# Eight-step, full-width products of x, with their shares kept in DRAM, for the GRU of a two-layer kernel

## The chip, the cores and the metric

The kernel runs on one core of a Trainium2 chip. The time is the device time of one execution in microseconds. Five engines work side by side, each on its own instruction stream: TensorE (PE in the profile, with its weight loads as PEld), VectorE (DVE), ScalarE (ACT), GpSimd (POOL) and SyncE (SP), which issues most DMA transfers.

## The reference

Two recurrent layers with residual additions, all in f32. The input x is 64 batches x 128 steps x 512 features, and a condition of 512 features belongs to each batch.

```python
# layer 0: gated linear recurrence, in closed form
f = sigmoid(x @ W_f.T + b_f);  i = sigmoid(x @ W_i.T + b_i)
f, i = f / (f + i + EPS), i / (f + i + EPS)
new = i * (x @ W_h.T + b_h)
log_cum = cumsum(log(f + EPS), axis=1)            # along the steps
scaling = exp(log_cum[:, -1:, :] - shifted_by_one(log_cum))
x = x + cumsum(scaling * new, axis=1) + exp(log_cum) * cond[:, None, :]

# layer 1: GRU, conditioned on cond
vz, vr, vh = cond @ C_z + b_z, cond @ C_r + b_r, cond @ C + b
def step(h, xt):
    z = sigmoid(xt @ W_z + h @ U_z + vz)
    r = sigmoid(xt @ W_r + h @ U_r + vr)
    hh = tanh(xt @ W + (r * h) @ U + vh)
    return (1 - z) * h + z * hh                   # from h = 0, output at every step
x = x + scan(step, x)
```

## The kernel before

**First layer.** 16 groups of four batches, and for each group four chunks of 128 features. TensorE forms the three gates of a chunk as 128-column matmuls over 512 tokens (`gate`, line 187). VectorE then divides, multiplies and scans along the steps. GpSimd adds the result to x (`add_hidden`), and SP writes it to the DRAM tiles `x2d`.

**Second layer.** The 64 batches are two streams of 32. A step of one stream has 32 batches as stationary columns, so one matmul uses a quarter of TensorE's width; four of them, for the four quarters q of the output features, stand side by side in four strips of 32 columns (`matmuls`, line 374). In a step (`Stream.step`, line 739) the bank `g` already holds the part of the three gates that comes from x and the condition. TensorE adds the r and z gates of the state (lines 749 to 754: one pass over 256 columns), ScalarE takes the sigmoid (755), VectorE multiplies r by h and transposes in 32x32 blocks (756, 757), TensorE adds the third gate (776), ScalarE takes the tanh (784), VectorE forms the new h and its transpose (791 to 799). The two streams alternate on TensorE, with stream 1 two steps behind.

**The x part.** Where `direct(st, t)` holds (the first 8 steps of stream 0, the first 4 of stream 1) `x_products` multiplies x by the weights in full. The other steps are done four at a time with fewer multiplications: the four steps and the feature halves make a 2x2 block product, done with seven multiplications instead of eight, and each of the seven is again a 2x2 block product of seven. This needs sums of blocks of x (`gather` puts them in `sums_to_take`, and GpSimd works them off at line 625) and differences of weights (line 420). `Outer` is one of the seven outer products; a `product` (line 542) is one inner product: four matmuls side by side in the four strips, 96 columns each. Of the seven inner products one lands in a small PSUM place (`spots`) that two blocks share (line 479), one in a spot that three blocks share (line 492), and results are carried on within the bank by ScalarE copies (487, 503). VectorE adds the shared part (516) and the outer terms (532), and the finished shares of four steps wait in SBUF (`xz`) until `put_share` (line 722) copies one to `g`. In the first groups some outer products are formed without the inner level (`plain`).

**Order.** Every compute instruction is pinned: the engines execute in the order of the program text. The loop at line 954 calls the steps of both streams in turn; `slots` says in which step an outer product begins, `first_visit` stands after the r and z gates of a step and `second_visit` after its third gate. Where a step has no products, `idle_products` multiplies zeros (line 630). DMA transfers go through SP's queue in the order in which the scheduler puts them: windows of eight steps of x (`load_window`, line 675: four transfers for each stream) and outputs (line 821: four transfers for four steps, in rows of 32 features). The features of a quarter are interleaved: quarter q holds features 128 j + 32 q + c.

Of the kernel before, what the change touches and what calls it, by code (L numbers as in the profile page):

```python
# [11 lines left out]
ALU = mybir.AluOpType  # L12
# [6 lines left out]
def kernel(  # L19
# [35 lines left out]

    nc = tc.nc
# [11 lines left out]
    HP = P // 2  # L68
# [33 lines left out]
    for tb in range(K):  # L102
        load_x(0, tb, tag="h", bufs=5)
    bias0 = const.tile([3 * K, P], F32, name="bias0")
# [97 lines left out]
    def add_hidden(g, c, x2=None, ts=slice(0, S)):  # L202
# [14 lines left out]
        if g == NG - 1 and ts.start == 0:  # L217
            pin(nc.scalar.copy(streams[1].windows[0][:, c, NG // 2 - 1], x2[:, : TW * GB]))
        return added

    def sums(g, c, ts=None):

        h, i = hidden[g, c], is_[c % 2]
        if ts is not None:
            h, i = by_batch(h)[:, :, ts], by_batch(i)[:, :, ts]
        return pin(nc.gpsimd.tensor_tensor(h, i, h, ALU.add))
# [27 lines left out]
    def chunk_norm(g, c, between=None):  # L254

        f, i = fs[c % 2], is_[c % 2]
        h = work.tile([P, NP], F32, tag="h", bufs=5, name=f"h_{g}_{c}")
# [11 lines left out]
        if g > 0 or c > 0:  # L269
            before = (g, c - 1) if c else (g - 1, K - 1)  # L270
            beside += [sums(*before), add_hidden(*before)]
# [39 lines left out]
    GATES = range(3)  # L311

    def load_weights(name, ws, tag):

        t = wpool.tile([P, K, 3, D], F32, tag=tag, name=name)
        for n, w in enumerate(ws):
            nc.sync.dma_start(t[:, :, n, :], w.rearrange("(k p) e -> p k e", p=P))
        return t

    def part(w, q):  # L320

        return w.rearrange("p g (j q c) -> p g j q c", q=Q, c=C)[:, :, :, q, :]
# [3 lines left out]
    def conditioning():  # L326

        for n, b_ in enumerate((b_r, b_z, b)):
            for q in range(Q):
                rows = b_.rearrange("(j q c) -> q j c", q=Q, c=C)[q]  # L330
                nc.sync.dma_start(
                    bias1[q * SB : (q + 1) * SB, n].rearrange("p (j c) -> p j c", c=C),
                    rows.partition_broadcast(SB),
                )
        cw = load_weights("cw", (C_r, C_z, C_h), "wa")
        ps = [psum.tile([P, 3, P], F32, tag="tp", name=f"pv{s}") for s in range(2)]
        for s in range(2):
            for k in range(K):
                for j in range(K):
                    for q in range(Q):  # L340
                        pin(
                            nc.tensor.matmul(
                                ps[s][q * SB : (q + 1) * SB, :, j * C : (j + 1) * C],
                                lhsT=condT[:, k, s * SB : (s + 1) * SB],
                                rhs=part(cw[:, k], q)[:, :, j],
                                start=(k == 0 and j == 0),
                                stop=(k == K - 1),
                                skip_group_check=True,
                            )
                        )  # L350
        vs = []
        for s in range(2):
            whole = const.tile([P, 3, P], F32, name=f"whole_v{s}")
            pin(nc.vector.tensor_tensor(whole, ps[s], bias1, ALU.add))

            v = const.tile([P, 3, HP], F32, name=f"v{s}")
            pin(nc.vector.tensor_tensor(v, whole[:, :, HP:], whole[:, :, :HP], ALU.subtract))
            vs.append((whole, v))
# [3 lines left out]
    RZ, HH = slice(0, 2), slice(2, 3)  # L362
    TW = 8
    HC = K // 2
    out_parts = out.rearrange("b t (j q c) -> q b t j c", q=Q, c=C)

    def matmuls(p, lhsT, w, start=True, stop=True, half=False):

        if half:
            p = p.rearrange("p g j c -> p g (j c)")  # L370
# [13 lines left out]
    def winograd_weights():  # L384
# [8 lines left out]
        quads = [((b11[k], b12[k]), (b21[k], b22[k]), t[:, :, k]) for k in range(HC)]  # L393
        return (b11, b21, b22, t1, t2, t3, t4), iter([d for q_ in quads for d in differences(*q_)])

    def differences(b1, b2, t):

        (b11, b12), (b21, b22) = b1, b2
        t1, t2, t3, t4 = (t[:, n] for n in range(4)) if not isinstance(t, list) else t
        return [(t1, b12, b11), (t2, b22, t1), (t3, b22, b12), (t4, b21, t2)]  # L400

    def quarters(w_):

        return [[w_[k][:, :, j * P : (j + 1) * P] for j in range(2)] for k in range(HC)]
# [8 lines left out]
    def take_inner(n, t):  # L413

        inner_weights[n] = t
        return differences(*quarters(w_products[OPERANDS[n][1]]), t)
# [4 lines left out]

    class Outer:
# [3 lines left out]
        count = 0  # L426

        def __init__(self, st, group, n, inner):
            self.st, self.group, self.n, self.inner = st, group, n, inner
            self.left, w_n = OPERANDS[n]  # L430
            self.w = quarters(w_products[w_n])
            if inner:
                self.t = inner_weights[n]
            self.r = banks[Outer.count % len(banks)]
            Outer.count += 1
            st.need_sums(group, self.left[0] == "s")

        def a(self, m, k):

            st, cols = self.st, slice(k * SB, (k + 1) * SB)  # L440
            if self.left[0] == "s":
                return st.s4[:, self.left[1], m, cols]
            _, i, j = self.left
            return st.x4[self.group % 2][:, 2 * i + m, j * HP : (j + 1) * HP][:, cols]

        def s(self, n):
            left = self.left
            return self.st.ss[:, n, 4 + left[1] if left[0] == "s" else 2 * left[1] + left[2]]

        def at(self, m, j):  # L450
            return self.r[:, m, :, j, :]

        def spot(self):
            spots.append(spots.pop(0))
            return spots[-1]

        def plain(self, m):
            for k in range(HC):
                matmuls(
                    self.r[:, m], lambda _: self.a(m, k), [self.whole_w(k)],  # L460
                    start=(m == 0 and k == 0), stop=(k == HC - 1), half=True,
                )

        def whole_w(self, k):
            return w_products[OPERANDS[self.n][1]][k]

        def first(self):
            self.common = None  # L470
            if not self.inner:
                return self.plain(0)
            self.p = self.spot()
            product(self.p, self.a(0, 0), self.w[0][0], start=True)

        def copy_first(self):
            if self.inner:
                p = self.p.unsqueeze(2).to_broadcast([P, 3, 2, C])
                pin(nc.scalar.copy(self.r[:, 0], p))  # L479

        def second(self):
            if self.inner:
                product(self.at(0, 1), self.s(1), self.t[1])

        def copy_second(self):
            if self.inner:
                pin(nc.scalar.copy(self.at(1, 0), self.at(0, 1)))

        def copy_shared(self, place):
            commons.append(commons.pop(0))  # L490
            self.common = commons[-1]
# [517 lines left out]
```

## Time and profile before

| | us |
|---|---|
| median of 3 runs (2013.69 to 2016.28) | 2015.03 |
| the profiled execution's own time | 2013.68 |
| its span | 2011.9 |
| the GRU's first matmul starts at | 711.2 |
| TensorE busy from 800 to 1975 us | 1132 of 1175 |
| VectorE busy from 800 to 1975 us | 760 |
| ScalarE busy from 800 to 1975 us | 580 |
| GpSimd busy from 800 to 1975 us | 708 |

The granted TensorE clock is 1.00 in every stage. An f32 matmul appears as two records of TensorE and two of its weight load. Matmuls are pipelined and the ends of their records are modelled, so that records overlap: the pace of TensorE is read from the starts. "issue" beside an idle time means that the engine waited for nothing that the profile shows.

### The profile page before, as it was taken

To read this page: it belongs to the slowest core of one execution; us is meant where nothing else is said; L and a number is where in the kernel's file an instruction comes from. 1 tells how busy PE (TensorE), PEld (TensorE's weight loads), DVE (VectorE), ACT (ScalarE), POOL (GpSimd) and SP (SyncE) were. 2 spreads that over 40 slices of the span, in tenths; PEclk is the share of its full clock that TensorE was granted. 3 is DMA by queue.
4 is the path that set the end of the run, shared out by engine and by line. 5 is a ranking of instruction groups with operands and counts; after the bars stand their busy time and mean duration, and the time that the engine had idled before them with its cause. 6 is when DMAs were issued, how large, how long until landed. Compare 5 with 4: busy or idle time off the path is not lost.

```text
span 2011.9 us, 96221 instructions
## 1 busy us (share of the span) xinstructions
PE 1949.9 (97%) x42665; PEld 1408.7 (70%) x42665; DVE 1486.9 (74%) x2992; ACT 765.9 (38%) x2770; POOL 940.8 (47%) x1824
## 2 busy tenths in 40 slices
PE   9999999999999989999999999999999999999998
PEld 5444444444444446888888888888888889888886
DVE  6899999999999965666666666666666666666664
ACT  3122121221222222554445454444554445544442
POOL 1222222222222244656665666566656655656562
DMA  6411111211111220211211212112112111120111
GB/s 203 154 48 47 42 53 44 77 53 42 48 47 47 54 41 11 38 25 31 41 26 26 40 21 35 27 30 41 26 31 36 30 26 32 25 40 15 20 20 19
DMA packets 295064, 86.15 MB, mean 43 GB/s; under 512 B 272044, under 2 KB 272056, under 8 KB 294648
## 3 DMA queue, kind: packets, MB, share of 16 engines
q1 hardware_dynamic: 294048, 79.92, 17.7%
q8 instruction: 335, 5.49, 1.2%
q14 instruction: 81, 0.66, 0.1%
q10 hardware_dynamic: 600, 0.07, 0.0%
HBM read 46.41 MB, written 33.55 MB: 40 GB/s over the span
## 4 chain that ended last, share of the span: by engine, by line
PE 71%; DVE 22%; issue 3%; POOL 2%; ACT 1%; DMA 1%; DVEq 0%; ACTq 0%; SPq 0%; POOLq 0%
PE g L374 35%; PE bank L542 17%; PE p L187 12%; DVE h L260 7%; PE spots L542 6%; DVE h L309 2%; DVE i L292 2%; DVE h L299 2%; DVE i L291 1%; DVE i L304 1%; DVE f L276 1%; DVE h L259 1%; DVE i L279 1%; PE bank L374 1%; POOL ss L625 1%
## 5 line engine op out<-in xcount | busy, mean ns | idle before, releaser
L187 PE MATMUL p<-xT,W 128*128 128x512 f32 (+1 forms) x1560 | 670.8, 586 | 2.1 <-ACT xT L146 1.7
L374 PE MATMUL g<-w_s,h 128*32 128x256 f32 x8128 | 521.1, 380 | 14.8 <-issue 11.9
L187 PEld LDWEIGHTS p<-xT,W 128*128 128x128 f32 x1560 | 289.7, 190 | 344.8 <-issue 334.7
L374 PEld LDWEIGHTS g<-w_s,h 128*32 128x32 f32 x8128 | 324.4, 110 | 108.4 <-issue 29.8
L374 PE MATMUL g<-w_s,f 128*32 128x128 f32 x8128 | 297.0, 273 | 16.4 <-issue 10.8
L756 DVE TENSOR_TENSOR f<-f,h 128x128 f32<-128x128 f32 x254 | 74.3, 292 | 294.3 <-ACT f L755 294.3
L542 PE MATMUL bank<-w_inner,ss 128*32 128x96 f32 x5712 | 267.4, 247 | 9.9 <-issue 6.3
L374 PEld LDWEIGHTS g<-w_s,f 128*32 128x32 f32 x8128 | 236.4, 110 | 29.4 <-issue 21.0
L264 POOL COPY first<-condT 128x4 f32<-128x4 f32 x64 | 12.1, 190 | 519.1 <-DVE h L259 504.1
L260 DVE RECIPROCAL h<-h 128x517 f32<-128x517 f32 x64 | 217.0, 3391 | 2.2
L759 POOL TENSOR_SCALAR f<-f 128x128 f32<-128x128 f32 x254 | 75.7, 298 | 303.4 <-DVE f L756 303.4
L278 ACT ACTIVATE f<-f 128x512 f32<-128x512 f32 x64 | 40.4, 631 | 448.3 <-DVE f L276 448.3
L801 POOL TENSOR_TENSOR o<-o,h 128x128 f32<-128x128 f32 x254 | 115.9, 456 | 200.7 <-DVE h L797 192.0
L542 PEld LDWEIGHTS bank<-w_inner,ss 128*32 128x32 f32 x5712 | 190.1, 110 | 19.9 <-POOL ss L625 10.0
L479 ACT COPY bank<-spots 128x192 f32<-128x192 f32 x416 | 131.0, 315 | 147.9 <-PE spots L542 122.3
L755 ACT ACTIVATE f<-g 128x256 f32<-128x256 f32 x254 | 97.4, 384 | 231.4 <-PE g L374 227.7
L784 ACT ACTIVATE h<-g 128x128 f32<-128x128 f32 x256 | 71.0, 277 | 282.6 <-PE g L374 282.6
L532 DVE TENSOR_TENSOR W<-bank,W 128x384 f32<-128x384 f32 x305 | 169.6, 557 | 10.4
L791 DVE TENSOR_TENSOR h<-h,f 128x128 f32<-128x128 f32 x254 | 85.1, 335 | 110.1 <-ACT h L784 109.5
L542 PE MATMUL spots<-w_inner,ss 128*32 128x96 f32 x2856 | 129.8, 246 | 0.3 <-issue 0.3
L760 POOL TENSOR_TENSOR f<-f,h 128x128 f32<-128x128 f32 x254 | 117.0, 461 | 21.2
L722 ACT COPY g<-W 128x384 f32<-128x384 f32 x244 | 123.7, 507 | 0.2
(142 smaller groups left out, 3738.7 us busy)
## 6 DMA issues: line engine op xcount, KB each, us to landing
x<-in_x_dram SPq DMA_DIRECT2D x64, 256.0 KB, 3.0
x2d<-x SPq DMA_DIRECT2D x63, 256.0 KB, 2.0
xw<-x2d SPq DMA_DIRECT2D x124, 128.0 KB, 4.3
out_dram<-o SPq DMA_DIRECT2D x248, 64.0 KB, 2.1
w_rows<-in_L_cond_W_f_dram SPq DMA_DIRECT2D x4, 256.0 KB, 5.1
w_rows<-in_L_cond_W_i_dram SPq DMA_DIRECT2D x4, 256.0 KB, 5.9
w_rows<-in_L_cond_W_h_dram SPq DMA_DIRECT2D x4, 256.0 KB, 5.5
w_s<-in_L_cond_U_r_dram SPq DMA_DIRECT2D x1, 1024.0 KB
```

What stands on the lines that cost most here:

```text
L187: nc.tensor.matmul(p[:, tokens], lhsT=W0[:, c, n, k, :], rhs=xT[g][:, k, tokens], start=(k == 0), stop=(k == K - 1),)
L260: pin(nc.vector.reciprocal(h, h))
L374: nc.tensor.matmul(p[q * SB : (q + 1) * SB], lhsT=lhsT(k), rhs=part(wk, q), start=(start and k == 0), stop=(stop and k == len(w) - 1), ski ...
L479: pin(nc.scalar.copy(self.r[:, 0], p))
L532: pin(nc.vector.tensor_tensor(dst, r, other, ALU.add))
L542: nc.tensor.matmul(out_[q * SB : (q + 1) * SB], lhsT=a, rhs=w_[:, :, q * C : (q + 1) * C], start=start, stop=True, skip_group_check=True,)
L722: pin(nc.scalar.copy(self.g, self.xz[:, t // 2 % 2, t % 2]))
L755: pin(nc.scalar.activation(rz, g[:, RZ], AF.Sigmoid))
L759: pin(nc.gpsimd.tensor_scalar(r, z, -1.0, 1.0, ALU.mult, ALU.add))
L760: pin(nc.gpsimd.tensor_tensor(r, r, h_, ALU.mult))
L791: pin(nc.vector.tensor_tensor(hh, hh, z, ALU.mult))
L801: pin(nc.gpsimd.tensor_tensor(o, o, h, ALU.add))
```

## The change

The products of x are cut differently. A group is now eight steps of all 64 batches: two halves of four steps by two halves of the features, and within each the same again. A block has 2 steps x 64 batches = 128 stationary columns, so an inner product is one matmul of full width, 128 x 384, instead of four in strips. Each of the four output blocks of an outer product has a PSUM bank of its own, and one more bank takes the shared part. Seven inner products p1 to p7 run through the banks as a chain: p1, p3 and p5 are each copied on to the next bank by ScalarE, and p2 is the shared one.

Output rows of a block are now (2 steps x 64 batches), while a step needs (4 quarters x 32 batches), so VectorE leaves finished shares in SBUF, SP stores them to DRAM, and each step loads its own share again one step ahead. `place` puts products into the steps until a target number is reached: once after the r and z gates, once after the third gate, and no second link of one chain in the same place. `idle_products` and `plain` are gone. The direct steps become 12 and 8.

In a step r and z are two passes of 128 columns with a sigmoid each. The output is added in transposed form by GpSimd, and is transposed back in the next step. Features of a quarter are now adjacent (128 q + e), which changes how weights, biases, x and outputs are loaded and stored. A window of x now covers both streams and takes 32 transfers. The piece of the last group's first window that comes from the last chunks goes from SBUF to SBUF by DMA instead of by ScalarE.

```diff
     def add_hidden(g, c, x2=None, ts=slice(0, S)):
...
         if g == NG - 1 and ts.start == 0:
-            pin(nc.scalar.copy(streams[1].windows[0][:, c, NG // 2 - 1], x2[:, : TW * GB]))
+            for j in range(K):
+                nc.sync.dma_start(
+                    windows[0, 1][j][c * C : (c + 1) * C, NG - 1], x2[j * C : (j + 1) * C, : TW * GB]
+                )
...
     def part(w, q):
-        return w.rearrange("p g (j q c) -> p g j q c", q=Q, c=C)[:, :, :, q, :]
+        return w[:, :, q * P : (q + 1) * P]
...
+    def load_window(w, s=None, groups=None):
+        first_, n = (0, NG) if s is None else (s * NG // 2, groups or NG // 2)
+        windows[w, s] = []
+        for j in range(K):
+            t = work.tile([P, NG, TW * GB], F32, tag="xw", bufs=4, name=f"xw{w}_{s}_{j}")
+            windows[w, s].append(t)
+            for s_ in range(2):
+                a, b_ = max(first_, s_ * NG // 2), min(first_ + n, (s_ + 1) * NG // 2)
+                if a >= b_:
+                    continue
+                for q in range(Q):
+                    nc.sync.dma_start(t[q * C : (q + 1) * C, a:b_], x2d[s_][...])
...
     class Outer:
...
-    def product(out_, a, w_, start=False):
-        for q in range(Q):
-            pin(nc.tensor.matmul(out_[q * SB : (q + 1) * SB], lhsT=a, rhs=w_[:, :, q * C : (q + 1) * C], ...))
+        def product(self, bank, a, w_, start=False):
+            pin(nc.tensor.matmul(banks[bank], lhsT=a, rhs=w_, start=start, stop=True, skip_group_check=True))
+
+        def continued(self, to, of):
+            def copy():
+                self.free(to)
+                pin(nc.scalar.copy(banks[to], banks[of]))
...
+            to_copy.append(copy)
...
+        def products(self):
...
+            def p1():
+                self.free((0, 0))
...
+                self.product((0, 0), self.a(0, 0), w_[0][0], start=True)
+                self.continued((0, 1), (0, 0))
+            def p3():
+                self.product((0, 1), self.s(1), t[1])
+                self.continued((1, 0), (0, 1))
...
+        def read(self, block):
...
+            if j == 1 or block == (1, 1):
+                pin(nc.vector.tensor_tensor(r, r, self.common, ALU.add))
...
+            pin(nc.vector.tensor_tensor(dst, r, other, ALU.add))
...
+    def place(target):
+        chained = set()
+        while state["placed"] < target and ahead:
+            o, f, chain = ahead[0]
+            if chain and o in chained:
+                break
+            ahead.pop(0)
+            f()
+            if chain:
+                chained.add(o)
+            state["placed"] += 1
...
     def direct(st, t):
-        return t < (8 if st.s == 0 else 4)
+        return t < (12 if st.s == 0 else 8)
...
+        def load_share(self, t):
+            self.share = work.tile([P, 3 * P], F32, tag="xz", bufs=2, name=f"xz{self.s}_{t}")
+            rows = shares_d[t // TW % len(shares_d)][t % TW, self.s]
+            nc.sync.dma_start(self.share, rows.rearrange("q b e -> (q b) e"))
...
     def step(self, t, ...):
+            copies()
+            if t + 1 < S and not direct(self, t + 1):
+                self.load_share(t + 1)
+            while to_store:
+                to_store.pop(0)()
...
-                matmuls(g[:, RZ], ..., [w_s[:, k, RZ] for k in range(K)], start=False)
-                pin(nc.scalar.activation(rz, g[:, RZ], AF.Sigmoid))
+                of_state(0, hT_)
+                of_state(1, hT_)
+                pin(nc.scalar.activation(r, g[:, 0], AF.Sigmoid))
                 pin(nc.vector.tensor_tensor(rh, r, h_, ALU.mult))
                 pin(nc.vector.transpose(rhT, rh))
+                pin(nc.scalar.activation(z, g[:, 1], AF.Sigmoid))
...
+            read(len(to_read))
...
+            place(targets[0])
...
-                matmuls(g[:, HH], ...)
-                idle_products(idle[1])
-            second_visit()
+                of_state(2, rhT)
+            copies()
+            place(targets[1])
             pin(nc.scalar.activation(hh, g[:, 2], AF.Tanh))
...
+    GOALS = ((7, 0), (15, 35), (26, 84), (16 * (NX - 1) - 6, 7 * 7 * (NX - 1) - 14), (16 * (NX - 1) + 2, 7 * 7 * (NX - 1)))
```

## The prediction

> **What bounds the kernel now.** I read the page first: shares of the engines, then the chain that ended last, then the costliest groups.
>
> ```profile
> span 2011.9 us, 96221 instructions
> PE 1949.9 (97%) x42665; PEld 1408.7 (70%) x42665; DVE 1486.9 (74%) x2992; ACT 765.9 (38%) x2770; POOL 940.8 (47%) x1824
> ...
> PE 71%; DVE 22%; issue 3%; POOL 2%; ACT 1%; DMA 1%; DVEq 0%; ACTq 0%; SPq 0%; POOLq 0%
> ```
>
> DVE's 22% is the first layer (its scans and reciprocals, to about 711 us), which the diff leaves alone. From 711 us on (1301 us, the GRU) the chain is TensorE alone, so I read that stage in order of time. A row of the timeline is start, length, engine, line, operation and count; the count is of records, two for each f32 matmul.
>
> ```profile
> 1304.84 0.38 PE L374 MATMUL g<-w_s,h 128*32 128x256 f32 x1
> ...
> 1306.56 0.57 PE L542 MATMUL bank<-w_inner,s 128*32 128x96 f32 x13
> ...
> 1307.84 0.29 PE L542 MATMUL bank<-w_x,ss 128*32 128x96 f32 x4
> ...
> 1308.01 0.29 PE L542 MATMUL bank<-w_x,s 128*32 128x96 f32 x4
> ...
> 1308.17 0.29 PE L542 MATMUL bank<-w_inner,ss 128*32 128x96 f32 x4
> ```
>
> Starts tell the pace, since ends overlap. The r and z gates of a step take 1306.56 - 1304.84 = 1.72 us; one product of x (four 32-column matmuls side by side) takes 0.165 us (1307.84, 1308.01, 1308.17); the third gate takes 0.88 us in the same way (1303.63 to 1304.51). A bare stream would be the same: the first layer's full-width matmul of 512 columns starts every 429 ns a record, so four strips of 96 columns side by side need 4 x 2 x 96 x 0.838 / 4 = 161 ns. Column strips already run four at once at 97% of the array's pace; using all 128 columns in one matmul has almost nothing left to win there.
>
> What TensorE loses is elsewhere, in stalls with no waiter:
>
> ```profile
> 1314.09 0.66 PE L374 MATMUL g<-w_s,h 128*32 128x256 f32 x8
> 1316.42 0.85 PE L374 MATMUL g<-w_s,h 128*32 128x256 f32 x12 [1.66 <-issue]
> ```
>
> From 800 to 1975 us there are 50 pauses over 0.6 us between TensorE instructions, 43 us together, and nearly every one has a 16 KB packet of the instruction queue that began 0.4 to 2.4 us before it. I read them as TensorE waiting for its own instructions.
>
> **The change, part by part.** Streaming work of TensorE in the second stage, by the paces above:
>
> - State gates: r and z become two passes of 128 columns instead of one of 256. 254 x 3 x 0.88 = 670.6 for 254 x (1.72 + 0.88) = 660.4: +10.2 us. In return r's sigmoid can start a pass earlier, which matters only where TensorE waits (the tail).
> - Direct x products: 12 + 8 steps instead of 8 + 4. Eight more at 2.58 us (741.14 to 743.72): +20.6 us.
> - Products: 416 inner blocks x 7 = 2912 at 0.1655 us, 11 plain blocks at 1.30 us and 116 idle matmuls (9.4 us) go, 505.6 us. 15 groups x 49 = 735 matmuls of 128 x 384 come, each 2 x 429 x 384/512 = 644 ns: 473.3 us. -32.3 us.
> - Three matmuls that preset banks: +1.9 us. Sum of streaming: +0.4 us. The same multiplications, differently shaped.
>
> **Switching width** is the new cost. Before, TensorE works in 32-column strips throughout the second stage. After, the state's gates stay in strips and the products are full width, placed after r/z and again after the third gate. In the order in which the changed kernel's instructions stand there are 468 runs of full-width products (209 of one, 251 of two, 8 of three), each between strips: 936 switches. The trace has one clean switch each way, with no unmet wait beside it:
>
> ```profile
> 63.67 0.87 PE L342 MATMUL pv<-cw,condT 128*32 128x96 f32 x31
> 64.46 0.70 PE L187 MATMUL p<-xT,W 128*128 128x512 f32 x1
> ...
> 64.46 0.30 PEld L187 LDWEIGHTS p<-xT,W 128*128 128x128 f32 x2
> ...
> 709.84 1.45 PE L187 MATMUL p<-xT,W 128*128 128x512 f32 x3
> 711.22 0.85 PE L374 MATMUL g<-w_s,zeros 128*32 128x384 f32 x8
> ```
>
> Strips to full: the last strips start at 64.28 and, at 82 ns a set, the next could start at 64.36. The full matmul starts at 64.46 together with its weight load, and its record is 0.70 instead of 0.59 long: the load is not hidden, streaming begins about 64.57. Loss 0.21 us. Full to strips: the last full one starts at 710.69, is through at 711.12, and the strips, whose second set follows at 711.56 one 0.32 us stream later, began at 711.24. Loss 0.12 us. A pair costs 0.33 us, 468 pairs 154 us.
>
> [...] Bounds: nothing[...] and 0.5 us a pair (234 us), if each switch waits out a whole 0.25 us strip record.
>
> **Instruction supply.** TensorE falls from 21,487 to 14,381 matmuls, each four instructions, and the densest stretch (16 instructions in 0.165 us) is gone. The stage's pauses (43 us) fall at least with the count (-36%, -16) and at most vanish (-43). I take -28.
>
> **Work moved off TensorE's path.** Per step DVE reads 630 blocks of 128x384 at 557 ns in all (351 us; before 427 x 557 + 416 x 343 ns = 380); ScalarE has 420 bank copies of some 507 ns (213 us) for 1664 of 232 to 315 (429 us); GpSimd's sums stay near 1.7 us a step. None reaches the 5.3 us that a step will take, so the work is covered by TensorE. Its order is not: a chain of seven products now holds three copies from bank to bank, and a product waits for the copy of the one before. The copy stands in ScalarE's queue ahead of r's sigmoid or the tanh, and can first need a bank read on DVE (two instructions, 1.1 us). From r's last matmul the third gate's input is ready in 1.0 us (sigmoid 0.28, product 0.29, transpose 0.31, hand-overs); TensorE gets there after 0.88 + 0.21 + 0.64 to 1.29 + 0.12 us, so 0.85 to 1.5 us are to spare. The gate loses up to 0.3 us where such a read is forced, on fewer than half the steps: 0 to 60 us, I take 12.
>
> **DMA.** SP issued 553 transfers, now 1462: each share is stored (128 x 1.5 KB) and loaded again per step, and a window comes as 32 transfers instead of 8.
>
> ```profile
> 1308.51 3.92 SPq L675 DMA_DIRECT2D xw<-x2d  x4
> ...
> xw<-x2d SPq DMA_DIRECT2D x124, 128.0 KB, 4.3
> out_dram<-o SPq DMA_DIRECT2D x248, 64.0 KB, 2.1
> ```
>
> A share is asked for at a step's start and copied to PSUM by ScalarE at its end, some 4 us later, against about 2 us to land. Queued behind it on SP are stores and window pieces; ahead of it too. If it is late, ScalarE's copy blocks the other stream's sigmoid, then its third gate. Eight small window pieces stand between two share loads, at some 0.4 us each 3.2 us. Range 0 to 42 us (1.5 us twice in each of 14 windows), I take 5. [...]
>
> **Junction and tail.** The last group's first window now goes SBUF to SBUF by DMA (2 us) and through 8 gathers before the first product of stream 1, where TensorE already waited 1.3 us: +3. Products end 12 paired steps before the end of stream 0, where each leaves about 0.5 us idle: +6; the three lone steps shorten by 1 us each, since r no longer waits for z: -3. Leaving out idle matmuls could drop the clock, which every stage shows at 1.00: [...] a lone step's longest pause here is 2003.25 - 2001.49 = 1.8 us: nothing[...].
>
> **Sum.** 0.4 + 154 - 28 + 12 + 5 + 6 = 149 us on the profiled execution's own 2013.7 (span 2011.9 and 1.8 around it), 2163; the median shown, 2015.0, is 1.3 above that execution: **2164 us**.
>
> **Rivals.**
> - *Switches are free* (10%): [...] 2164 - 154 = 2010, faster, and some 1990 with the waits at nothing. Speaks for it: the weight queue runs ahead of matmuls in all of the first layer. Against: at the one switch it didn't. It decides below 0.01 us a pair with my other terms, below 0.05 with no waits.
> - [...]
> - *Bank copies become the wait* (12%): 0.25 us more in each of 254 steps, 2164 + 64 = 2228. For: each chain link passes TensorE, ScalarE and sometimes DVE. Against: a step's engines are under 75% full.
> - *Shares come late by SP* (8%): 2164 + 37 = 2201. Against: the loads are asked for a step ahead.
> - *The forecast* (55%), its own range 2125 to 2200.
>
> No change within 0.2% (about what a measurement of this kernel can tell) is a narrow band, 2011 to 2019, between the first rival and the rest: 2%. Faster 10%, slower 88%. The range leaves out the free switch below, and the worst of the waits above: 2055 to 2255.
>
> **What would show it.** A step of about 5.3 us (before 4.85); full-width products starting 0.2 us after the strips before them with their weight load beside them, and 0.64 us apart within a run; strips 0.12 us late after them; fewer pauses laid to issue. It is wrong if first full products of a run follow at the strips' own pace, or if TensorE's waits name a bank copy or a share.

## The result, and the profile after

The changed kernel takes 2231.41 us (median of 4 runs, 2230.39 to 2233.42), the kernel before 2014.36 us beside it: a ratio of 1.108, with a 95% interval of 1.1061 to 1.11. It is slower, as forecast; the forecast was 2164, so 67 us are missing. That is inside the range (2055 to 2255), but above the 2125 to 2200 that the prediction gave to its own mechanism.

The head of the page after, and the shares of the chain that ended last, which answer to the lines of before:

```profile
span 2228.9 us, 68043 instructions
PE 2085.5 (94%) x28453; PEld 1230.5 (55%) x28453; DVE 1496.5 (67%) x2778; ACT 680.5 (31%) x1848; POOL 878.8 (39%) x1572
...
PE 59%; DVE 27%; DMA 4%; SPq 3%; ACT 3%; issue 3%; POOL 0%; DVEq 0%; ACTq 0%; POOLq 0%
```

TensorE issues a third fewer instructions and is busy 136 us longer in a span 217 us longer. New on the chain are transfers and SP's queue (4% and 3%), which stood at 1% and 0% before. Most of SP's part is the first layer, which the forecast left alone; of the transfers, about half (`DMA shares<-W`, 2% by the page) are stores of shares in the second.

The timeline after, with TensorE and the engines that follow it (start, length, engine, line, operation, count of records; in brackets the idle time before and who ended it):

```profile
1504.89 1.96 PE L365 MATMUL g<-w_s,h 128*32 128x128 f32 x64
1506.77 0.30 PEld L495 LDWEIGHTS bank<-w_t,x 128*128 128x128 f32 x2 [0.20 <-issue]
1506.77 0.91 PE L495 MATMUL bank<-w_t,x 128*128 128x384 f32 x2
1506.91 0.28 ACT L747 ACTIVATE f<-g 128x128 f32<-128x128 f32 x1 [1.25 <-PE g L365]
1507.08 0.27 ACT L750 ACTIVATE f<-g 128x128 f32<-128x128 f32 x1
...
1507.55 0.31 DVE L749 STREAM_TRANSPOSE f<-f 128x128 f32<-128x128 f32 x1
1508.01 1.08 PE L365 MATMUL g<-w_s,f 128*32 128x128 f32 x32 [0.32 <-DVE f L749]
1509.02 0.91 PE L495 MATMUL bank<-w_inner,inner_sum 128*128 128x384 f32 x2
...
1509.77 0.81 PE L495 MATMUL bank<-w_t,inner_sum 128*128 128x384 f32 x2
1510.50 1.19 PE L365 MATMUL g<-w_s,h 128*32 128x128 f32 x36
```

The r and z gates stream for 1.72 us, so they could be done at 1506.61 (0.838 ns a column and record, four strips at once); the full-width product starts at 1506.77 with its weight load beside it. Two products follow each other in 0.75 us, 0.11 above the bare stream of 0.644, and the strips after them 0.73 us later. These are the switches as forecast. Not as forecast is the third gate at 1508.01: it waits for VectorE's transpose, because r's sigmoid (L747) starts at 1506.91, when z too is done, and not a pass earlier.

What ended TensorE's waits from 800 to 2180 us (total us, times, longest):

```profile
PE g L365 <- DVE f L749: 46.3, 104, 1.2
PE bank L495 <- ACT bank L503: 17.0, 39, 0.8
PE bank L495 <- DVE W L580: 12.7, 15, 2.0
ACT g L709 <- DMA xz<-shares: 11.5, 12, 1.4
```

A step of one stream takes (2121.26 - 973.77) / 204 = 5.63 us, by the tanh of steps 28 and 232 counted over both streams; the forecast had 5.3. It put the step before at 4.85, where the same count gives 5.00.

The first of the waits listed is that for r. Copies from bank to bank and reads of banks are the second and third; late shares cost ScalarE little. The waits of TensorE laid to issue, 37.5 us between 800 and 1975 us before, are gone.

**Where 217 us went.** For each run of like matmuls I take the time from its start to the start of the next, less its bare stream; what is left is lost time. Summed from the first to the last tanh, with the rest of that stretch as bare stream:

| | before | after | difference |
|---|---|---|---|
| GRU's first matmul at | 711.2 | 738.4 | +27.2 |
| bare stream of the GRU | 1173.4 | 1178.1 | +4.7 |
| lost time | 117.4 | 302.7 | +185.3 |

That is 217.2 us; the spans differ by 217.0. The rows add up by the way they are made: they say where time goes, not what would be saved if a cause were gone.

### The profile page after: what moved, and what is told of

Read it like the earlier page. It is cut to its first block, busy times and chain, and to the rows that moved or that the text cites. A ratio compares the mean times of both kernels' runs of the same rounds, so it can differ in the third digit from the quotient of the medians.

```text
span 2228.9 us, 68043 instructions
## 1 busy us (share of the span) xinstructions
PE 2085.5 (94%) x28453; PEld 1230.5 (55%) x28453; DVE 1496.5 (67%) x2778; ACT 680.5 (31%) x1848; POOL 878.8 (39%) x1572
## 4 chain that ended last, share of the span: by engine, by line
PE 59%; DVE 27%; DMA 4%; SPq 3%; ACT 3%; issue 3%; POOL 0%; DVEq 0%; ACTq 0%; POOLq 0%
PE g L365 31%; PE bank L495 16%; PE p L188 9%; DVE h L264 6%; DVE h L313 2%; DVE i L296 2%; DVE h L303 2%; SPq L322 2%; DMA shares<-W 2%; DVE f L749 2%; DVE W L580 2%; DVE f L748 2%; ACT f L747 2%; PE banks L495 2%; DVE bank L576 1%
## 5 line engine op out<-in xcount | busy, mean ns | idle before, releaser
L365 PEld LDWEIGHTS g<-w_s,h 128*32 128x32 f32 x16256 | 430.1, 110 | 133.3 <-issue 127.4
L365 PE MATMUL g<-w_s,h 128*32 128x128 f32 x16256 | 496.4, 274 | 4.6 <-DVE h L792 4.6
L795 POOL TENSOR_TENSOR h<-h,x 128x128 f32<-128x128 f32 x254 | 118.9, 468 | 379.9 <-DVE h L792 332.8
L785 DVE TENSOR_TENSOR h<-h,f 128x128 f32<-128x128 f32 x254 | 104.0, 409 | 218.5 <-ACT h L779 217.2
L503 ACT COPY bank<-bank 128x384 f32<-128x384 f32 x315 | 145.9, 463 | 283.6 <-DVE W L580 223.5
L580 DVE TENSOR_TENSOR W<-bank,W 128x384 f32<-128x384 f32 x420 | 223.8, 542 | 12.5 <-DMA shares<-W 5.1
L264 DVE RECIPROCAL h<-h 128x517 f32<-128x517 f32 x64 | 217.0, 3391 | 2.2
L747 ACT ACTIVATE f<-g 128x128 f32<-128x128 f32 x254 | 70.5, 277 | 387.0 <-PE g L365 382.6
L495 PE MATMUL bank<-w_inner,inner_sum 128*128 128x384 f32 x330 | 146.7, 526 | 13.7 <-ACT bank L503 13.6
L779 ACT ACTIVATE h<-g 128x128 f32<-128x128 f32 x256 | 71.1, 278 | 252.5 <-PE g L365 252.3
L790 DVE TENSOR_TENSOR h<-h,f 128x128 f32<-128x128 f32 x252 | 112.6, 447 | 26.6 <-DVE h L785 0.5
L709 ACT COPY g<-xz 128x384 f32<-128x384 f32 x236 | 113.9, 483 | 18.6 <-DMA xz<-shares 11.5
L576 DVE TENSOR_TENSOR bank<-bank,x 128x384 f32<-128x384 f32 x210 | 115.0, 548 | 0.0
```

The source lines that it names most:

```text
L264: pin(nc.vector.reciprocal(h, h))
L365: nc.tensor.matmul(p[q * SB : (q + 1) * SB], lhsT=lhsT(k), rhs=part(wk, q), start=(start and k == 0), stop=(stop and k == len(w) - 1), ski ...
L495: nc.tensor.matmul(banks[bank], lhsT=a, rhs=w_, start=start, stop=True, skip_group_check=True)
L503: pin(nc.scalar.copy(banks[to], banks[of]))
L576: pin(nc.vector.tensor_tensor(r, r, self.common, ALU.add))
L580: pin(nc.vector.tensor_tensor(dst, r, other, ALU.add))
```

## The experiments

All are edits of the changed kernel. It took 2231.4 and, repeated on a second chip, 2232.0 us, while the kernel before took from 1987 to 2014 on the chips of these runs. I therefore compare with 2232.0, in us, and give the ratio to the kernel before beside it. That the other versions are as steady from chip to chip is taken over from this one kernel: e1 to e4 ran on one chip, c_after and e5 to e7 on a second, e8 and e9 on a third, e10 and e11 on a fourth.

| run | what | us (median of 4) | against 2232.0 | ratio to before, 95% |
|---|---|---|---|---|
| c_after | changed kernel again | 2232.02 | | 1.1232 (1.1196 to 1.1268) |
| e1_spread | weight loads spread | 2201.87 | -30.2 | 1.1056 (1.1038 to 1.1074) |
| e2_strips | products in strips | 2173.13 | -58.9 | 1.0906 (1.0887 to 1.0926) |
| e4_half | half of them in strips | 2214.35 | -17.7 | 1.1115 (1.1097 to 1.1134) |
| e3_split | added wait between r and z | 2234.03 | +2.0 | 1.1226 (1.1202 to 1.1249) |
| e5_rbank | r in its own bank | 2156.94 | -75.1 | 1.085 (1.0814 to 1.0886) |
| e6_rbank_strips | e5 and e2 | 2110.76 | -121.3 | 1.0614 (1.0566 to 1.0663) |
| e7_all | e6 and e1 | 2083.07 | -149.0 | 1.0474 (1.0434 to 1.0513) |
| e8_windows_act | e7, windows of x on ScalarE's queue | 2127.84 | -104.2 | 1.0595 (1.0574 to 1.0617) |
| e9_full | e8 at full width | 2200.20 | -31.8 | 1.096 (1.0929 to 1.0991) |
| e10_windows8 | e7, windows in 8 transfers | 2160.95 | -71.1 | 1.0862 (1.0823 to 1.0901) |
| e11_win_full | e10 at full width | 2241.41 | +9.4 | 1.1267 (1.1242 to 1.1292) |

### The chip, or the kernel

> The changed kernel itself, unchanged, beside the three that follow, on the same chip. The kernel before has shown 1991 us on one chip and 2014 us on another. If the difference of chips lies in something that only the kernel before has (its pauses for instructions), this run shows 2231 within 4 us whatever the chip; if the chips differ in pace, it moves with the kernel before, by about 1%.

It took 2232.02 us where the kernel before took 1987.32. So the chips differ in the kernel before and not in this one. Its pauses for instructions are the part of it that the changed kernel lacks, and they would fit; no trace of the kernel before on that chip was read, so that is argued only.

### The first layer

In the changed kernel the weights w_s and w_x are twelve transfers of 256 KB each on SP's queue, where they were three of 1 MB. The chain of waits of the changed kernel from 0 to 140 us (start, length, what):

```profile
34.57 2.55 SPq L322
37.16 2.55 SPq L322
39.75 2.55 SPq L322
42.34 2.55 SPq L322
45.00 12.88 DMA x<-in_x_dram
...
105.29 2.45 SPq L217
...
108.28 10.03 DMA x<-in_x_dram
```

The first four weight pieces are issued in 2.8 us, and from then on most hold SP for 2.55 us each (256 KB in 2.55 us is 103 GB/s), about the pace of the transfers themselves. The x of the first layer stands behind them: it is asked for at 45.0 us, where it was at 29.7.

```diff
-                    nc.sync.dma_start(t[:, j, n, :], w.rearrange(...)[j])
+                    weight_pieces.append(lambda ...: nc.sync.dma_start(t[:, j, n, :], w.rearrange(...)[j]))
...
         pin(nc.vector.reciprocal(h, h))
+        if g > 0:
+            for _ in range(2 if g < 3 else 1):
+                if weight_pieces:
+                    tie(weight_pieces.pop(0)(), total)
```

> The changed kernel with one thing different: the 24 pieces of 256 KB of the weights w_x and w_s are not issued in two blocks of twelve, but one or two at a time, each after the first vector instruction of a later chunk of the first layer. Theory (the first layer's x waits behind blocked weight loads in SP's queue): the GRU's first matmul comes back from 738.4 to 711 to 714 us, the reciprocals in groups 0 and 1 run on at some 10.8 us a chunk, and the time falls by 24 to 28 us, 2231 to about 2205. Rival (the loads are hidden and the 27 us come from something else, such as the way the pieces are read): the first matmul stays at 735 or later and the time within 5 us of 2231.

It gained 30.2 us. VectorE's fourth reciprocal (55.13 us in the kernel before), and the GRU's first matmul, in the timelines of the changed kernel and then of this run:

```profile
72.89 3.39 DVE L264 RECIPROCAL h<-h 128x517 f32<-128x517 f32 x1
...
738.43 0.85 PE L365 MATMUL g<-w_s,zeros 128*32 128x384 f32 x8
```

```profile
54.97 3.39 DVE L264 RECIPROCAL h<-h 128x517 f32<-128x517 f32 x1
...
708.91 0.85 PE L371 MATMUL g<-w_s,zeros 128*32 128x384 f32 x8
```

The theory holds: the pieces of the weights, issued in one block, cost the first layer its 27 us, and all of it reaches the end. The block is long because the pieces are slow. Two stretches show it, the changed kernel while SP is held, and the kernel before while it loads the same w_s (the last three figures: granted clock, busy share of the DMA engines, GB/s):

```profile
27.00:45.00 18.00, 14.78 (x53) 7.65 (x51) 14.63 (x12) 5.68 (x10) 5.40 (x6) 1.00 0.26 98
...
23.00:31.00 8.00, 8.00 (x29) 4.25 (x28) 6.07 (x7) 2.81 (x5) 0.59 (x2) 1.00 0.99 357
```

At 357 GB/s the 3 MB of w_s would have passed in some 9 us (an estimate from this row). The size of a piece is not what slows it: from 6 to 14 us, where the changed kernel loads x and its first weights in 256 KB transfers too, it moves 349 GB/s. What in the new layout leaves three quarters of the DMA engines idle was not tested; in e1 the pieces are as slow (82 GB/s from 72 to 76 us), but nothing stands behind them.

### The switches

```diff
-            pin(nc.tensor.matmul(banks[bank], lhsT=a, rhs=w_, start=start, stop=True, ...))
+            for q in range(Q):
+                pin(nc.tensor.matmul(banks[bank][q * SB : (q + 1) * SB],
+                                     lhsT=a[..., q * SB : (q + 1) * SB], rhs=w_, start=start, stop=True, ...))
```

> The changed kernel with each full-width product of x (128x384, 0.644 us) formed as four 32-column strips side by side (32x384 each, the same streaming time), in the same places, with the same banks, copies, reads and transfers: only the switch of width is gone. Theory (the switches cost about 0.36 us a pair, 468 pairs): the time falls by 150 to 185 us, 2231 to about 2063, and a product follows the gates with less than 0.05 us lost. Rival (the loss at these places is the wait for banks, copies and sums, or is fixed by the chain r, sigmoid, third gate): under 40 us gained, above 2190. Between them, some of the gap turns into the wait for r's sigmoid after lone products: 2080 to 2130.

> The changed kernel with only those products in strips that stand between the r/z gates and the third gate; those after the third gate stay full width. Switches per half step fall from two pairs to one. Theory (a fixed price of each pair, whatever its place): half the gain of the version in which all are strips, 75 to 92 us of some 168, so about 2147. Rival (what costs is the exposed wait ahead of the third gate, and the pairs after it are free): nearly the whole gain, above 140 us. Opposite rival (the pairs ahead of the third gate only eat into a wait that is there anyway): under 40 us.

In e4_half the strips are used only between the r/z gates and the third gate. The gains are 58.9 and 17.7 us, far under both theories. The first fits none of the cases named for it; the second fits the opposite rival, that the pairs ahead of the third gate eat into a wait that is there anyway. The lost time by place shows why; us between steps 64 and 224, counted over both streams, with the median of one in brackets:

| from, to | changed (c_after) | strips (e2) | half (e4) |
|---|---|---|---|
| r/z, product | 26.9 (0.168) | 7.6 (0.031) | 8.8 (0.055) |
| product, r/z | 41.1 (0.20) | 15.3 (0.003) | 41.2 (0.20) |
| third gate, product | 31.1 (0.153) | 19.0 (0.012) | 36.1 (0.153) |
| one product, third gate | 46.1 (0.648) | 67.3 (0.778) | 54.0 (0.761) |
| two products, third gate | 28.5 (0.201) | 28.1 (0.188) | 22.9 (0.119) |
| all | 173.7 | 136.7 | 162.9 |

The price of a switch is there and goes where the strips go: (0.168 - 0.031) + (0.20 - 0.003) = 0.334 us for a pair around r/z, and about the same after the third gate (0.153 - 0.012 there in place of the first term). The strips take away the change of width and the full-width weight load together, so these two are not told apart. But ahead of the third gate the loss grows by what the switch gave up. From the end of r/z to the third gate with one product between is 0.168 + 0.644 + 0.648 = 1.46 us with the switches and 0.031 + 0.644 + 0.778 = 1.45 without: something else sets that time.

### The chain of r

My first explanation was that r's sigmoid waits for the whole run of matmuls, since r and z stand in one without a wait between.

```diff
-                of_state(1, hT_)
+                of_state(1, hT_, last_on_pool[0])
```

> The changed kernel with one wait added: z's first matmul waits for a GpSimd instruction of the half step before, which is long done, so that TensorE reports r's 16 matmuls before it begins z's (in 222 of 254 half steps[...]). Theory (r's sigmoid starts only when z is done, and the third gate then waits after a lone product): the sigmoid of r starts about 0.85 us earlier, the third gate's waits for the r-times-h chain (46 us) go, and the time falls by 35 to 48 us, to about 2188. Rival (the wait is set by something behind the sigmoid, such as VectorE's queue of bank reads): under 10 us gained. A third outcome: the added wait itself stops TensorE, and the time rises.

It gained nothing (+2.0 us), and the sigmoid did not move; timeline of that run:

```profile
1506.07 1.95 PE L365 MATMUL g<-w_s,h 128*32 128x128 f32 x64
...
1507.96 0.91 PE L497 MATMUL bank<-w_t,x 128*128 128x384 f32 x2
1508.10 0.28 ACT L751 ACTIVATE f<-g 128x128 f32<-128x128 f32 x1 [1.25 <-PE g L365]
```

The sigmoid still comes 2.03 us after the start of r. In the instructions it still waits for z's last matmul (z's own sigmoid, L754, carries no wait any more): r and z are columns of one PSUM tile. So that explanation was not shown, and the run said nothing on the theory. The next kept the added wait and gave r a tile of its own, in a PSUM bank of its own; ScalarE fills r's part of a share with a copy of its own in the other stream's next step.

```diff
+    r_bank.append(psum.tile([P, 3, P], F32, tag="p2", name="r_bank"))
...
+            r_place = g[:, 0] if t == 0 or direct(self, t) else r_bank[0][:, self.s]
...
-                pin(nc.scalar.activation(r, g[:, 0], AF.Sigmoid))
+                pin(nc.scalar.activation(r, r_place, AF.Sigmoid))
...
-            pin(nc.scalar.copy(self.g, self.share...))
+            pin(nc.scalar.copy(self.g[:, 1:], share[:, 1:]))
+            r_to_put.append((self, put_r))     
```

> The changed kernel with the r gate in a PSUM bank of its own (both streams in one bank; ScalarE fills r's part of the share in the next half step, one small copy more a step) and the added wait of the run before. The run before left the start of r's sigmoid where it was, since the sigmoid still waited for z's last matmul: r and z lay in one PSUM tile. Now it waits for r's last. Theory (after a lone product the third gate waits for r's sigmoid, 0.45 us beyond what a switch costs, 98 times): r's sigmoid starts about 0.85 us earlier, the third gate's excess after one product falls from 0.65 to about 0.2 us, and the time falls by 38 to 50 us against the changed kernel on the same chip. Rival (the chain is set behind the sigmoid, by VectorE's queue or the bank copies): under 10 us.

It gained 75.1 us. The timeline of this run:

```profile
1501.86 1.08 PE L365 MATMUL r_bank<-w_s,h 128*32 128x128 f32 x32
...
1502.75 1.06 PE L365 MATMUL g<-w_s,h 128*32 128x128 f32 x32
1503.00 0.28 ACT L762 ACTIVATE f<-r_bank 128x128 f32<-128x128 f32 x1 [1.17 <-PE r_bank L365]
...
1503.64 0.31 DVE L764 STREAM_TRANSPOSE f<-f 128x128 f32<-128x128 f32 x1
1503.74 0.91 PE L497 MATMUL bank<-w_t,sum 128*128 128x384 f32 x2
...
1505.23 1.08 PE L365 MATMUL g<-w_s,f 128*32 128x128 f32 x32
```

r's sigmoid starts 1.14 us after r does, 0.89 earlier than before, while z still streams; whether the shared tile or the shared bank held it back is not told apart. The third gate's loss after one product falls from 0.648 to 0.198 us (median), as expected. In the 160 steps the loss is 125.4 us for 173.7. Of the 48 us, 29 are after one product and 9 after two; the other 10 are waits of products for banks and copies. Outside that stage 5 us are gained before step 28, 11 from there to step 64, and 11 in the tail, where a lone step waits for the same chain. The gain is larger than expected because I had counted the lone products only.

> The run with r in its own bank, with all products in strips as well. Products in strips alone gave some 58 us where the count of switches promised 168; in that run the third gate waits 0.96 us after a lone product. Theory (the lost switches were hidden behind the chain of r, so that the two losses overlap and only both together give their sum): 130 to 165 us below the changed kernel, at 2065 to 2100, with the third gate's excess after one product under 0.15 us. Rival (switches were never worth more than 58, and the rest of the loss is in banks and copies): 58 plus the gain of r's bank alone, some 105 us at most.

Together 121.3 us: above what the rival allows, and below the theory's 130. The medians say that the switches and the chain are gone (after one product 0.001 us), but the mean there is about 0.5 us, in a few long waits. What ended them, from 1150 to 1950 us:

```profile
ACT g L720 <- DMA xz<-shares: 95.3, 37, 5.3
DVE W L588 <- DMA shares<-W: 33.4, 17, 2.6
PE g L365 <- DVE f L770: 27.2, 9, 3.7
```

The shares, late by at most 1.4 us in the changed kernel, are now late by up to 5.3. That the shorter step makes SP's queue matter is the reading that the next runs try. Where nothing is late, a step takes 4.55 to 5.7 us here; 5.63 is the mean of the changed kernel (900.9 / 160) and 5.00 that of the kernel before (799.6 / 160).

> The run before with the weight loads of the first layer spread as well. Theory (the first layer's delay is independent of the second layer): 27 to 31 us below the run before, about 2050. This is then the changed kernel without its three losses, still above the kernel before by the eight more direct steps (20.6 us), the slow start of the GRU and bank waits. Rival (the first layer's time is given back at the start of the GRU, where windows of x are late): under 15 us.

27.7 us below e6, so the first layer's loss stands apart from the rest. This is the fastest version made, and it is 4.7% slower than the kernel before on the same chip; what is left of the difference was not taken apart.

### SP's queue, two attempts

```diff
-                    nc.sync.dma_start(t[q * C : (q + 1) * C, a:b_], x2d[s_][...])
+                    x_pieces.append(lambda dst=dst, src=src: pin(nc.scalar.dma_start(dst, src)))
```

> The version with strips, r in its own bank and spread weights, in which the windows of x from the third on (and half of the second) are issued by ScalarE, two pieces at a time after the sigmoids and after the share's copy, instead of by SP. In the run before, ScalarE waits 95 us for shares between 1150 and 1950 us, up to 5.3 us at once, where SP's queue holds window pieces and outputs ahead of the share loads, while an undisturbed step takes 4.55 us. Theory (SP's queue is what limits once the switches and the chain of r are gone): those waits fall below 30 us and the time falls by 60 to 110 us, from 2083 to about 2000, near the kernel before. Rival (the shares are late because they are stored late, or the pieces delay ScalarE's sigmoids as much): within 20 us of 2083.

> The same with the products full width again: the changed kernel with r in its own bank, spread weights and windows issued by ScalarE. The difference to the strips beside it is the price of the switches with the other waits out of the way. Theory (0.33 to 0.37 us a pair, 468 pairs): 2110 to 2130, some 120 to 170 us above the strips. Rival (overlap remains, the slower step hides what the strips lose to SP): under 60 us above the strips, as in the first pair.

Here the windows are also begun seven steps earlier. The first is 44.8 us slower than e7 in place of faster. Waits of e8 in the same stage:

```profile
ACT bank L527 <- DMA xw_None<-x2d: 40.5, 17, 3.1
ACT f L784 <- DMA xw_None<-x2d: 38.1, 12, 4.5
ACT g L736 <- DMA xz<-shares: 31.4, 15, 4.5
```

The waits for shares fall from 93.5 us to 31.4, nearly as the theory has it, and ScalarE now waits in its own queue at its own transfers (40.5 and 38.1 us), with the sigmoids behind them. That is the rival's mechanism, at more than twice the loss it allowed. The next run lays x out in DRAM so that a window is 8 transfers and not 32, on SP.

```diff
-    x2d = [dram.tile([NG // 2, K, P, NT], F32, ...) for s in range(2)]
+    x2d = [dram.tile([NG // 2, K, Q, C, NT], F32, ...) for s in range(2)]
...
-                for q in range(Q):
-                    nc.sync.dma_start(t[q * C : (q + 1) * C, a:b_], x2d[s_][...].rearrange("g c n -> c g n"))
+                nc.sync.dma_start(t[:, a:b_], x2d[s_][..., j, :, :, ...].rearrange("g q c n -> (q c) g n"))
```

> The version with strips, r in its own bank and spread weights (2083 us), in which x after the first layer lies in DRAM so that a window of eight steps is 8 transfers of 128 KB on SP's queue instead of 32 of 32 KB; nothing is moved to ScalarE. The run with windows on ScalarE cut the waits for shares from 95 to 31 us (1150 to 1950 us), but put its own transfer waits into ScalarE's queue (some 80 us) and was slower. Theory (the shares are late behind the number of window pieces in SP's queue): waits for shares fall below 35 us, nothing comes in their place, and the time falls by 50 to 90 us, to about 2010, level with the kernel before. Rival (the shares are late because their stores and the outputs fill the queue, whatever the windows do): within 15 us of 2083.

> The same with full-width products: the changed kernel with its first layer, its r gate and its windows mended, and the switches left in. Theory (a pair of switches costs 0.335 us net once nothing else waits, 468 pairs, 157 us, of which what is left of the waits in the strips' version is to be taken off): 2105 to 2130, that is 80 to 130 us above the strips beside it. Rival (the switches stay hidden behind other waits): under 50 us above.

Both times miss: e10 is 77.9 us slower than e7, and the shares are later still (1150 to 1950 us):

```profile
ACT g L725 <- DMA xz<-shares: 142.7, 29, 9.3
```

Fewer transfers, each held longer: from 1200 to 1840 us SP spends 95 us on 60 pieces, the longest 4.57 us, where e7 spends 141 us on 238 pieces, the longest 1.77. A share behind one of these waits longer. Neither attempt settles which work on SP should go; that stays open.

The two pairs price the switches a third and a fourth time. Full width against strips costs 58.9 us in the changed kernel, 46.2 with r mended (e5 to e6), 72.4 with windows on ScalarE (e8 to e9) and 80.5 with large windows (e10 to e11): in no setting the 157 that 468 pairs of 0.335 us make. The third is under e9's theory (120 to 170), the fourth at the lower edge of e11's (80 to 130).

Long waits cost twice here, since TensorE's granted clock fell with them (in the changed kernel to 0.51 after a wait of 2.00 us, read below): from 1150 to 1950 us its mean is 1.00 in c_after and e5, 0.99 in e2, 0.98 in e6 and 0.95 in e10. Half of TensorE's busy time in the half-clock stretches of the GRU comes to some 5 us in c_after, 14 in e2, 4 in e5, 24 in e6, 29 in e8, 23 in e9, 41 in e10 and 43 in e11 (an estimate from the one trace of each). With that taken off, the four prices of the switches are some 67, 66, 78 and 79 us, closer together than as measured.

## Why the prediction was right, and where it was short

**Direction and bound.** Right: TensorE is the bound (94% busy) and the strips were already at the full array's pace (97% of it, 161 ns for 165). The bare stream moved by +4.7 us where the sum had +0.4.

**Switches, 154 us.** The price was read rightly from two places of the trace: 0.33 us forecast, 0.334 measured, and 0.37 if the transitions of strips to strips are not taken off. From strips to a full-width product the loss is 0.168 us where strips to strips lose 0.031, and on the way back 0.20 where they lose 0.003 (medians). But the sum treated this loss as standing alone. Where one product stands between r/z and the third gate (99 times), the switches lie inside the 1.46 us of r's chain and taking them away gains nothing there; elsewhere the strips run into banks and shares. What removing them gained was 46 to 80 us, so 154 was too much for what they cost.

**"r's sigmoid can start a pass earlier", 0.85 to 1.5 us to spare.** This step failed. The sigmoid waits for z, so after a lone product the third gate came 0.45 us late beyond the switch, 99 times, some 46 us, and making the sentence true gained 75 (e5). I had 12 us here, for bank copies and order; the copies and reads did show as waits of TensorE (17.0 and 12.7 us), so that term was a little small as well.

**"The first layer, which the diff leaves alone."** This failed too: +27.2 us, from a line of the diff that I read as layout only, and e1 won it back. The same change of shape, 3 transfers to 12, was in the part on DMA only for the second layer.

**Instruction supply, -28.** The sign was right and the size short: no wait of TensorE's matmuls is laid to issue after 800 us, so the pauses (43 us) seem to have gone entirely, the far end of the range.

**Shares +5.** Right in this kernel (ScalarE waits 11.5 us for them, at most 1.4 at once); it becomes the limit only when the rest is mended.

**Junction +3, tail +3.** The tail was nearly even: the last 31 steps take 146.7 us for 149.9, though r waits for z there as well. The junction was not; timeline of the changed kernel:

```profile
778.24 0.91 PE L495 MATMUL bank<-w_x,x 128*128 128x384 f32 x2
788.94 1.65 PE L495 MATMUL banks<-w_inner,inner_sum 128*128 128x384 f32 x2 [9.79 <-POOL inner_sum L662]
```

The sums of the first group need the second window of x. SP issues its 32 transfers from 765.8 to 783.4 us, ScalarE has the last of them copied at 787 us, and only then GpSimd can form the sums: a stall of 9.8 us that the forecast did not have.

**The clock, nothing.** The clock did fall, though not in the lone steps, where the forecast looked for it: with pauses of up to 1.55 us it stays at 1.00 there, to the last matmul. From 711 us on the mean granted clock is 0.99. It is 0.50 from 786 to 790 us, in the stall just named, and it falls once in the middle of the GRU, after a wait of 2.00 us (timeline, then the row of that stretch with clock, DMA share and GB/s at its end):

```profile
945.96 1.59 PE L495 MATMUL bank<-w_t,sum 128*128 128x384 f32 x2 [2.00 <-DVE W L580]
947.34 1.49 PE L495 MATMUL banks<-w_inner,inner_sum 128*128 128x384 f32 x2
948.76 1.40 PE L365 MATMUL g<-w_s,f 128*32 128x128 f32 x32
...
946.00:949.40 3.40, 3.40 (x16) 1.67 (x20) 2.65 (x6) 0.46 (x1) 3.40 (x6) 0.51 0.06 9
```

The products stand 1.38 us apart in place of 0.75. The kernel before had pauses of up to 1.8 us and 1.00 throughout; what decides when the clock falls was not shown. In the changed kernel this costs some 3.5 us of the GRU, an estimate made as above: near the forecast's nothing in size, but the two waits behind it, 9.8 and 2.00 us, the forecast did not have.

In sum, by place: 27 (first layer), 46 (r's chain) and 10 (second window) are the missing terms, 83 us, and the pauses gave back 15 more than forecast; that is 68 of the 67 missing. The close fit is bookkeeping, since the smaller terms were not measured one by one. By what the runs gained it reads otherwise: taking away the switches gave 59 us, the first layer 30 and r's wait 75, all three together 149. So that the number lies in the range is in part luck: the switches were counted at more than twice what they cost alone, and this stood in for two losses, some 105 us, that the forecast had at nothing. The rival that came nearest in its number, bank copies at 2228 us, named the wrong wait: most of it was for r.

## What to carry to other kernels

Count the switches between column strips and full width before widening matmuls: here a pair costs a third of a microsecond where it stands, a third to a half of it came back when it was gone, and full width had almost nothing to win over four strips side by side, which ran at 97% of its pace. Two losses at one place were a maximum here, not a sum (1.46 us with the switches, 1.45 without): ask what chain would set that time if the loss were gone, and check in the instructions what a wait really waits for, since r, in one PSUM tile with z, was not early here: its sigmoid came 2.03 us after r's start (e3), and 1.14 with a tile and a bank of its own (e5). A load laid out anew is a change to every transfer behind it on that queue, in stages that the change was not about (27.2 us of the first layer here): compare its GB/s and the busy share of the DMA engines before and after.

## What the runs showed of the hardware

Four 256 KB transfers of the weights are issued in 2.8 us, and further ones hold SP for 2.55 us each; they move 98 GB/s with 0.26 of the DMA engines busy, where the same 3 MB in three transfers moved 357 GB/s. After a wait of TensorE of 2.00 us the granted clock was 0.51 for 3.4 us. The kernel before took from 1987 to 2014 us on different chips, and the changed one 2231.4 and 2232.0. Moving small transfers to ScalarE's queue cost its compute 79 us of waits in 800, more than the 62 us of waits for shares (93.5 in e7, 31.4) that it took away, and four times fewer, four times larger window transfers raised the waits for shares to 142.7 us.
